# Layer 1's experts: moving where pieces of attention stand inside a batch of experts

## The chip, the core and the metric

The kernel runs on one core of one Trainium2 chip. The metric is device time in microseconds (us), from the first to the last instruction and what lies around them, for one execution of the whole two-layer program. The core has a matrix engine (PE, with weight loads shown apart as PEld), a vector engine (DVE), an activation engine (ACT), a general engine (POOL) and a queue engine (SP) that issues most transfers. Each engine takes its instructions in the order in which the program was written for it.

## The reference

The input is x, 16 x 256 tokens of 128 numbers. Each of two layers normalises x, computes attention and a mixture of experts from the same normalised x, and adds their product to x. Layer 0 has gated linear attention and 8 experts; layer 1, where the change lies, has causal softmax attention with 16 heads and 16 experts, two of them for each token:

```python
mag = jnp.einsum('td,ndh->tnh', fx, bank_mag)
freq = jnp.einsum('td,ndh->tnh', fx, bank_freq)
hidden = jnp.tanh(mag) * jnp.cos(jax.nn.softplus(freq) + 0.1 + bank_phase[None, :, :])
out_all = jnp.einsum('tnh,nhd->tnd', hidden, bank_down)
...
x = x + s * g      # s: attention of layer 1, g: silu of the weighed experts
```

## The kernel before, in words

**Experts.** Tokens are sorted by expert on the chip and padded to 79 slots of 128 rows. A slot has one expert. `experts` takes a batch of 8 slots, so there are ten batches, numbered 0 to 9 here; the last has 7. One batch goes through these steps, in program order:

1. *Turning*: two groups of four transposes (L1133) into a PSUM tile `pxt`, each copied by ACT to `xgT` (L1135).
2. *Chain stage*: for each of four pairs of slots, 8 matmuls into `pf` (L1144), three ACT steps for softplus (L1149 to L1151) and five DVE steps that bring the angle into range (L1153 to L1161).
3. *Tanh stage*: a table of activation functions is loaded (L1165); for each pair, 8 matmuls into `pm` (L1171) and a tanh (L1177); then the sines of all four pairs (L1182; the cosine's quarter turn is in the phase), and the other table is loaded back (L1183).
4. *Product stage*: tanh times cosine on DVE (L1188), the choice of each row's weight (`weigh`, L393), then two halves of 16 matmuls into `pe` (L1196), each evacuated by DVE to `og` (L1201).

**Attention as filling.** `attention` is a generator of 254 pieces, and `fill(n)` emits the next n of them at the place where it is called. The pieces are: a *score pair* (`both`; in its full form the query scores `Sq` of one block, L940 and L946, together with the key scores `Sk` of an earlier block, L979), `queries` (L1008, L1010), `weighted` (L1029), `normed` (L1041), `turned` (L1061), `projected` (L1069), and for every four blocks a `setup` of two key parts (L911), two query parts (L902) and the values (L920). Two kinds of follow-up work are put off. The DVE step of most pieces (for a score pair the row maximum, L956 or L958) waits in the list `later` and is emitted when the next piece is taken. A score pair's exponential on ACT (L986) comes as an item of its own, kind 1, just before the next piece.

In a batch the calls are: one piece between the two groups of transposes; three in each of the four pairs of the chain stage, called the first, second and third place here (after the matmuls, after the ACT steps, after the DVE steps); at most one after each group of tanh matmuls; one after the second table load; and one after each half of the products. In the tanh stage `fill(1, False)` takes nothing as long as an exponential is due, because the table for it isn't loaded:

```python
if kind == 1 and not exps:
    ahead.append((kind, f))
    return True
```

So once a score pair has been taken there, no more is taken, and its exponential runs just after the load of L1183.

**PSUM.** The score tiles have the tag `S` and two buffers: in a full score pair `Sq` takes one and `Sk` the other. The next pair's `Sq` waits for the row maximum of this one, its `Sk` for this one's exponential. The other pieces share two buffers of the tag `ps`, and everything of the experts (`pxt`, `pf`, `pm`, `pe`) two of the tag `pf`.

**Other queues.** Each call of `fill` also calls `spread`, which issues one gather of rows (`xg`, L386) or one scatter of results (`yd`, L398) on POOL; POOL also masks the exponentials (L989). The weights of the next batch (`wt`, L1116) are issued on SP after a batch has been emitted; nine buffers serve batches of eight.

**The tail.** After the ten batches the remaining results are scattered (`give`), and a loop takes three pieces of attention and one step of `weighed` (L1211 to L1227) until all eight blocks of tokens are out (`finished`, L1233 to L1235). In one round of this loop a new block's results `gg` are loaded, and the blocks before it move on by a step:

```python
while b < NB:
    fill(3)
    next(ends, None)
```

Of the kernel before, what the change touches and what calls it, by code (L numbers as in the profile page):

```python
# [38 lines left out]
FILL = 3  # L39
# [13 lines left out]
def ib(ap, n):  # L53
    s = list(ap.shape)
    return ap.unsqueeze(len(s)).to_broadcast(s + [n])
# [3 lines left out]
def two_layer_kernel(  # L59
# [331 lines left out]
    def weigh(xg, lay, j0, n):  # L391

        return nc.vector.copy_predicated(  # L393
            xg[:, :n, D], seconds[lay][:, j0 : j0 + n].bitcast(I32), xg[:, :n, D + 1]
        )
# [44 lines left out]
    def spread():  # L440

        turn[:] = [not turn[0]]
        if wanted and (turn[0] or not given):
            fetch(1)
        else:
            give(1)
# [397 lines left out]
    with ExitStack() as c1:  # L844
# [281 lines left out]
        def experts(j0, n, wts, xg, fill):  # L1126

            vs, ths, xgTs = [], [], []
            for i0 in range(0, n, 4):
                n4 = min(4, n - i0)  # L1130
                pt = pf_.tile([P, 4, P], F32, tag="pf", name="pxt")
                for i in range(n4):
                    nc.tensor.transpose(pt[:, i, :], xg[:, i0 + i, 0:D], ident)  # L1133
                xgT = hp.tile([P, 4, P], F32, tag="xgT", name="xgT", bufs=3)
                nc.scalar.copy(xgT[:, 0:n4, :], pt[:, 0:n4, :])  # L1135
                xgTs.append(xgT)
                if i0 == 0:
                    fill(1)
            for i0 in range(0, n, 2):
                m = 2 * min(2, n - i0)  # L1140
                pf = pf_.tile([P, 4, P], F32, tag="pf", name="pf")
                for k in range(m):
                    i, c = i0 + k // 2, k % 2
                    nc.tensor.matmul(  # L1144
                        pf[:, k, :], wts[i][:, c * P : (c + 1) * P], xgTs[i // 4][:, i % 4, :], start=True, stop=True
                    )
                fill(1)
                z = hp.tile([P, 4, P], F32, tag="z", name="z", bufs=2)
                nc.scalar.activation(z[:, :m, :], pf[:, :m, :], AF.Abs)  # L1149
                nc.scalar.activation(z[:, :m, :], z[:, :m, :], AF.Exp, scale=-1.0)  # L1150
                nc.scalar.activation(z[:, :m, :], z[:, :m, :], AF.Ln, bias=1.0)  # L1151
                fill(1)
                nc.vector.scalar_tensor_tensor(z[:, :m, :], pf[:, :m, :], 0.0, z[:, :m, :], ALU.max, ALU.add)  # L1153
                v = hp.tile([P, 4, P], F32, tag="v", name="vt", bufs=CPB // 2 + 1)
                for i in range(m // 2):
                    ks = slice(2 * i, 2 * i + 2)
                    nc.vector.scalar_tensor_tensor(  # L1157
                        v[:, ks, :], z[:, ks, :], INV2PI, ib(wts[i0 + i][:, WROW - 2 :], P), ALU.mult, ALU.add
                    )
                nc.vector.tensor_scalar(z[:, :m, :], v[:, :m, :], MAGIC, MAGIC, ALU.add, ALU.subtract)  # L1160
                nc.vector.tensor_tensor(v[:, :m, :], v[:, :m, :], z[:, :m, :], ALU.subtract)  # L1161
                vs.append(v)
                fill(FILL - 2)

            nc.scalar.preload_act_table_set(TRIG)  # L1165
            for i0 in range(0, n, 2):
                m = 2 * min(2, n - i0)
                pm = pf_.tile([P, 4, P], F32, tag="pf", name="pm")
                for k in range(m):
                    i, c = i0 + k // 2, k % 2  # L1170
                    nc.tensor.matmul(  # L1171
                        pm[:, k, :], wts[i][:, H1 + c * P : H1 + (c + 1) * P], xgTs[i // 4][:, i % 4, :],
                        start=True, stop=True,
                    )
                fill(1, False)
                th = hp.tile([P, 4, P], F32, tag="th", name="th", bufs=CPB // 2 + 1)
                nc.scalar.activation(th[:, :m, :], pm[:, :m, :], AF.Tanh)  # L1177
                ths.append(th)
            for i0 in range(0, n, 2):
                m = 2 * min(2, n - i0)  # L1180
                v = vs[i0 // 2]
                nc.scalar.activation(v[:, :m, :], v[:, :m, :], AF.Sin, scale=TWOPI)  # L1182
            nc.scalar.preload_act_table_set(LN_EXP)  # L1183
            fill(1)
            for i0 in range(0, n, 2):
                m = 2 * min(2, n - i0)
                v, th = vs[i0 // 2], ths[i0 // 2]
                nc.vector.tensor_tensor(th[:, :m, :], th[:, :m, :], v[:, :m, :], ALU.mult)  # L1188
            weigh(xg, 1, j0, n)
            og = hp.tile([P, n, D], F32, tag="og", name="og", bufs=1)  # L1190
            for i0 in range(0, n, 4):
                n4 = min(4, n - i0)
                pe = pf_.tile([P, 4, D], F32, tag="pf", name="pe1")
                for i in range(i0, i0 + n4):
                    for c in range(2):
                        nc.tensor.matmul(  # L1196
                            pe[:, i - i0, :], ths[i // 2][:, 2 * (i % 2) + c, :],
                            wts[i][:, 2 * H1 + c * D : 2 * H1 + (c + 1) * D], start=(c == 0), stop=(c == 1),
                        )
                fill(1)  # L1200
                nc.vector.tensor_tensor(  # L1201
                    og[:, i0 : i0 + n4, :], pe[:, 0:n4, :], ib(xg[:, i0 : i0 + n4, D], D), ALU.mult
                )
                given.extend((og, 1, j0 + i, i) for i in range(i0, i0 + n4))
# [41 lines left out]
        def fill(n, exps=True):  # L1246

            k = 0
            while k < n:
                spread()  # L1250
                kind, f = ahead.pop() if ahead else next(pieces, (3, None))
                if kind != 1:
                    while later:
                        later.pop(0)()
                if kind == 3:
                    return False
# [3 lines that stand above are left out]
                if f is not None:  # L1260
                    f()
                k += kind == 0
            return True

        ET = mybir.EngineType
        with tc.manual_schedule(engines={ET.Activation, ET.PE, ET.DVE, ET.SP}):
# [20 lines left out]
            for k, (j0, n) in enumerate(batches):  # L1287
                now, got = got, None
                if k + 1 < len(batches):
                    got = rows_of(*batches[k + 1])  # L1290
                experts(j0, n, *now, fill)
                fetch(len(wanted))
                if got:
                    got = weights_of(*batches[k + 1]), got
# [61 lines left out]
```

## Time and profile before

| what | value |
|---|---|
| median of 3 runs | 1118.82 us (1113.76 to 1123.27) |
| profiled execution, own time | 1121.9 us |
| span of its instructions | 1120.2 us |
| granted PE clock, mean over the span | 0.874 of full speed |
| first tanh-stage table load to the last batch's one | 657.3 to 1021.7 us |
| last `og` of the experts ends | 1031.9 us |

The span is the time from the first to the last instruction on the core; 1.7 us lie around it in the profiled execution. "Idle before" in a row is the time in which an engine had nothing running just before that instruction, with the instruction that released it behind the arrow. Times in a timeline count from the start of the span.

### The profile page before, as it was taken

What the parts mean: (1) busy time and instruction counts of PE and PEld (TensorE: products, weight loads), DVE (VectorE), ACT (ScalarE), POOL (GpSimd) and SP (SyncE); (2) the same over time, 40 slices, a digit from 0 to 9 for tenths busy, and PEclk for the clock granted to TensorE, in tenths of its full rate; (3) what the DMA queues carried; (4) which work ended last, traced back from release to release, by engine and by line L of the source; (5) the groups of instructions that cost most, each with busy time, mean ns of one, the idle gap of its engine ahead of it and who ended that gap; (6) DMA issues with size and microseconds to landing.
All of it is one profiled execution on the core that took longest, in us unless ns stands there. A gap on an engine that the chain in (4) does not pass through costs nothing.

```text
span 1120.2 us, 17719 instructions
## 1 busy us (share of the span) xinstructions
PE 865.9 (77%) x6394; PEld 610.8 (55%) x6394; DVE 743.6 (66%) x1384; ACT 603.8 (54%) x1101; POOL 427.4 (38%) x446
## 2 busy tenths in 40 slices
PE   5545688788888878467867789888998888879676
PEld 4323466666666666335434366665666566656343
DVE  5677456646565655355688578778777866856585
ACT  3303566757657675364313365656565565545474
POOL 2000453544443622452121526445644643532220
PEclk9987799999989899656868799999999998988866
DMA  4040478633322320310070113432442343230241
GB/s 125 1 76 1 124 182 177 136 87 88 95 75 81 93 78 18 101 57 1 1 169 35 34 50 107 138 101 66 147 135 61 113 137 92 72 102 10 85 114 37
DMA packets 88416, 95.41 MB, mean 85 GB/s; under 512 B 22229, under 2 KB 64041, under 8 KB 88329
## 3 DMA queue, kind: packets, MB, share of 16 engines
q1 hardware_dynamic: 78632, 74.32, 24.1%
q0 software_dynamic: 9696, 19.97, 6.8%
q8 instruction: 50, 0.82, 0.3%
q14 instruction: 38, 0.30, 0.1%
HBM read 78.03 MB, written 22.51 MB: 90 GB/s over the span
## 4 chain that ended last, share of the span: by engine, by line
PE 42%; DVE 27%; ACT 17%; issue 7%; DMA 3%; POOL 3%; SPq 0%; DVEq 0%; POOLq 0%; ACTq 0%
PE pq L556 4%; PE Sq L946 4%; PE pf L737 3%; PE Sk L979 3%; PE pm L1171 3%; PE pe L1196 3%; DVE negm L958 2%; DVE vt L1157 2%; PE pe L767 2%; PE yx L1029 2%; PE Sq L940 2%; ACT pr L986 2%; DVE vt L1161 2%; DVE z L1153 1%; ACT sg L742 1%
## 5 line engine op out<-in xcount | busy, mean ns | idle before, releaser
L398 POOL DMA_INDIRECT yd<-og,row x150 | 157.4, 1049 | 236.0 <-DVE og L771 123.6
L386 POOL DMA_INDIRECT xg<-xnd,tok x150 | 150.2, 1001 | 111.1 <-ACT sp L522 53.3
L989 POOL TENSOR_SCALAR_AFFINE_SELECT pr<-pr 128x1024 f32<-128x1024 f32 x64 | 74.6, 1166 | 220.8 <-ACT pr L986 220.5
L979 PE MATMUL Sk<-qm,kT 32*128 32x256 f32 x768 | 130.1, 464 | 28.4 <-DVE negm L958 25.9
L986 ACT ACTIVATE pr<-Sk 128x1024 f32<-128x1024 f32 x96 | 97.9, 1021 | 78.6 <-PE Sk L979 78.3
L946 PE MATMUL Sq<-km,qT 32*128 32x256 f32 x768 | 130.0, 458 | 8.8 <-DVE mx L956 6.9
L737 PE MATMUL pf<-xgT,wt 128*128 128x128 f32 x568 | 82.8, 293 | 26.4 <-ACT sg L745 8.6
L946 PEld LDWEIGHTS Sq<-km,qT 32*128 32x128 f32 x768 | 71.6, 209 | 56.1 <-issue 33.4
L979 PEld LDWEIGHTS Sk<-qm,kT 32*128 32x128 f32 x768 | 77.0, 216 | 42.2 <-DVE negm L958 29.1
L737 PEld LDWEIGHTS pf<-xgT,wt 128*128 128x128 f32 x568 | 75.9, 205 | 43.6 <-issue 16.4
L958 DVE TENSOR_REDUCE negm<-Sq 128x8 f32<-128x1024 f32 x64 | 78.0, 1220 | 30.6 <-PE Sq L946 16.0
L742 ACT ACTIVATE sg<-pf,nb 128x128 f32<-128x128 f32 x142 | 44.1, 362 | 61.5 <-PE pf L737 61.3
L940 PE MATMUL Sq<-mq,identb 128*128 128x512 bf16 x128 | 43.5, 425 | 22.6 <-DVE negm L958 11.0
L753 DVE SCALAR_TENSOR_TENSOR gt<-pf,nb,sg 128x128 f32<-128x128 f32 x142 | 42.4, 343 | 21.0 <-ACT sg L746 21.0
L1196 PE MATMUL pe<-wt,th 128*128 128x128 f32 x316 | 42.2, 289 | 16.7 <-DVE th L1188 16.7
L1196 PEld LDWEIGHTS pe<-wt,th 128*128 128x128 f32 x316 | 39.0, 200 | 24.1 <-DVE th L1188 13.0
L956 DVE TENSOR_REDUCE mx<-Sq 128x8 f32<-128x1024 f32 x32 | 39.0, 1218 | 13.0 <-PE Sk L979 8.5
L618 DVE COPY_PREDICATED a<-upper,pA 128x512 f32<-128x512 int32 x32 | 23.3, 729 | 35.3 <-PE pA L617 34.5
L355 ACT ACTIVATE ohj<-hi,place 128x568 bf16<-128x568 bf16 (+1 forms) x16 | 12.7, 795 | 61.8 <-DVE hi L354 58.7
L1144 PE MATMUL pf<-xgT,wt 128*128 128x128 f32 x316 | 44.4, 284 | 0.0
L1144 PEld LDWEIGHTS pf<-xgT,wt 128*128 128x128 f32 x316 | 39.8, 196 | 8.2 <-issue 8.0
L767 PE MATMUL pe<-sb_wo,gt 128*128 128x128 f32 x284 | 38.1, 287 | 7.5 <-DVE gt L753 7.2
(273 smaller groups left out, 2066.0 us busy)
## 6 DMA issues: line engine op xcount, KB each, us to landing
wt<-bank SPq DMA_DIRECT2D x79, 385.0 KB
wt<-in_w_dram SPq DMA_DIRECT2D x71, 256.0 KB
gg<-yd SPq DMA_DIRECT2D x32, 256.0 KB
xnd<-xnx SPq DMA_DIRECT2D x16, 260.0 KB
xg<-xnd,tok POOLq DMA_INDIRECT x150
yd<-og,row POOLq DMA_INDIRECT x150
x<-in_x_dram SPq DMA_DIRECT2D x8, 256.0 KB
bank<-in_freq_dram SPq DMA_DIRECT2D x1, 2048.0 KB
```

The lines of the kernel that those rows point to most:

```text
L386: return nc.gpsimd.indirect_dma_start(out=xg[:, i, :], out_offset=None, in_=xnds[lay], in_offset=bass.IndirectOffsetOnAxis(ap=toks[lay][:, ...
L398: give = nc.gpsimd.indirect_dma_start(out=yds[lay], out_offset=bass.IndirectOffsetOnAxis(ap=rows[lay][:, j : j + 1], axis=0), in_=og[:, i, ...
L737: nc.tensor.matmul(pf[:, c, :], wts[i][:, c * P : (c + 1) * P], xgT[:, i, :], start=True, stop=True)
L767: nc.tensor.matmul(pe[:, i, :], gts[i][:, c, :], sb_wo0[:, c, :], start=(c == 0), stop=(c == 1))
L940: nc.tensor.matmul(S[:, c], identb, mq, start=True, stop=False, skip_group_check=True)
L946: nc.tensor.matmul(S[:, c, js, :], qT[part][r, tq], km[r, js, tk], start=not diag, stop=True, skip_group_check=True,)
L958: passed(nc.vector.tensor_reduce(ng, S, AX.X, ALU.max, negate=True))
L979: nc.tensor.matmul(S[:, c, js, :], kT[part][r, tk], qm[r, js, :], start=True, stop=True, skip_group_check=True,)
L986: nc.scalar.activation(pr, S, AF.Exp, scale=scale)
L989: pooled(nc.gpsimd.affine_select(pr_, pr_, pattern=[[0, 8], [1, P]], compare_op=ALU.is_ge, fill=0.0, base=0, channel_multiplier=-1,))
L1144: nc.tensor.matmul(pf[:, k, :], wts[i][:, c * P : (c + 1) * P], xgTs[i // 4][:, i % 4, :], start=True, stop=True)
L1196: nc.tensor.matmul(pe[:, i - i0, :], ths[i // 2][:, 2 * (i % 2) + c, :], wts[i][:, 2 * H1 + c * D : 2 * H1 + (c + 1) * D], start=(c == 0), ...
```

## The change

Three calls of `fill` change inside `experts`. One piece is added after the first four transposes, ahead of their copy; one is added between tanh times cosine and the products' matmuls; and in the first of the four pairs of the chain stage the third place is left out. A batch thereby has one fixed place more than before. No arithmetic changes.

```diff
                 for i in range(n4):
                     nc.tensor.transpose(pt[:, i, :], xg[:, i0 + i, 0:D], ident)
+                if i0 == 0:
+                    fill(1)
                 xgT = hp.tile([P, 4, P], F32, tag="xgT", name="xgT", bufs=3)
                 nc.scalar.copy(xgT[:, 0:n4, :], pt[:, 0:n4, :])
...
                 vs.append(v)
-                fill(FILL - 2)
+                if i0:
+                    fill(FILL - 2)
...
             weigh(xg, 1, j0, n)
+            fill(1)
             og = hp.tile([P, n, D], F32, tag="og", name="og", bufs=1)
```

`FILL` is 3, so `fill(FILL - 2)` takes one piece.

## The prediction

> **What bounds the kernel now.** I read the page's busy times first, then the waits of the matrix engine between 640 and 1030 us (the experts of layer 1), then windows by stage, then the timeline around one tanh stage, and last the tail.
>
> ```profile
> PE 865.9 (77%) x6394; PEld 610.8 (55%) x6394; DVE 743.6 (66%) x1384; ACT 603.8 (54%) x1101; POOL 427.4 (38%) x446
> ```
>
> ```profile
> PE pe L1196 <- DVE th L1188: 16.7, 9, 6.7
> PE Sk L979 <- DVE negm L958: 14.6, 8, 3.1
> PE Sq L940 <- DVE mx L956: 7.3, 5, 3.2
> ```
>
> The columns are total us, times, longest. PE waits for tanh times cosine ahead of the products (nearly 1.1 us a batch, but 6.75 once), and for row maxima in the chain stage. Nine chain stages (batches 1 to 9) together, by windows:
>
> ```profile
> sum 204.40, PE 174.99 PEld 116.06 DVE 172.56 ACT 125.09 POOL 138.99; mean PE 19.44 PEld 12.90 DVE 19.17 ACT 13.90 POOL 15.44
> ```
>
> There PE is busy 86% and DVE 84%: they bound the stage together, through the short score buffers. In the tanh and product stages ACT's fixed order and then PE decide.
>
> **What moves.** I counted the pieces through the code's order, from the first piece in batch 0 that the timeline shows (`normed` at 629.81). Before, a batch takes 1 + 12 + 1 + 2 = 16 fixed pieces, and the tanh stages take 8 in all: 168, leaving 37 for the tail. After, 17 fixed ones, and 6 in the tanh stages: 176, leaving 29. So eight pieces leave the tail: a `projected`, four score pairs (two with a mask), a `queries`, a `weighted`, a `normed`.
>
> **Their work in the experts.** At full clock the timeline has a masked pair at 1.7 us of PE, an unmasked one at 1.1, `projected` 1.0, `queries` 0.9, the short `weighted` 0.9, `normed` 0.5: 3.4 + 2.2 + 1.0 + 0.9 + 0.9 + 0.5 = **8.9 us** of PE, where PE is nearly full.
>
> **The new place before the products.** Batch 2 before, ACT and then PE:
>
> ```profile
> 747.44 1.28 ACT L1183 ACT_TABLE_LOAD   x1
> 748.73 1.02 ACT L986 ACTIVATE pr<-Sk 128x1024 f32<-128x1024 f32 x1
> ```
>
> ```profile
> 746.64 2.05 PE L1196 MATMUL pe<-wt,th 128*128 128x128 f32 x16 [0.93 <-DVE th L1188]
> 748.63 0.70 PE L946 MATMUL Sq<-km,qT 32*128 32x256 f32 x4
> 749.81 0.48 PE L979 MATMUL Sk<-qm,kT 32*128 32x256 f32 x2 [0.48 <-ACT pr L986]
> ```
>
> The products start 0.8 us before the sines end, and a score pair behind them still waits 0.48 us for the exponential that stands behind the table load. With a pair ahead of the products, that wait comes 2 us earlier: PE is free at 745.7, can do 0.35 us of `Sq`, and stands until 749.8; pair and first half then end near 753.0 instead of 751.0. Products, the gathers' release and everything behind on PE queue behind it. By the count the new place holds a score pair in batches 0, 2, 3, 7 and 9, always with an exponential pending. That loses 1.9, 2.0, 2.0, 1.9 and, where nothing was idle before (batch 9: products started at once at 1027.42, the exponential ended at 1030.29), 3.3: 11.1 us. Elsewhere the piece fits the gap: batch 1 (a key part) gains 1.0, batch 4 (`weighted`) 1.5, batch 5 (`queries`) 1.1. The 6.75 us wait of batch 8 is a key part in the place after the load: its copy waits behind load and exponential on ACT, and DVE's `km` (6.36 us idle) stands ahead of tanh times cosine. After the change that key part falls into batch 6, and a query part fills 1 us of it: 2.0 gained over both. Sum: 11.1 - 5.6 = **+5.5 us**. Bounds: -5.6, if no pair had to wait, to +11.1 without the gains; I take the worked value, since batch 2's row is the very wait.
>
> Two rules of the Trainium skill bear here. "ScalarE: Activation LUTs", "What ACT_TABLE_LOAD costs", has about 1.28 us for the load and 1.38 more for a drain. The rows above show 1.28 and the next activation 0.01 us after it. By the rule each of the five pairs would wait 1.38 longer, 6.9 in all; I use the row.
>
> The second speaks of the clock. PE stands still about 3.0 us (batches 0, 7), 3.3 (9) and 3.9 (2, 3). "TensorE: Matmul & The Clock Gate", "HAM oscillation", says gaps up to about 3.4 us keep the full clock. In this trace gaps of 1.75 us (804.34 to 806.09) and 3.21 (732.49 to 735.70) were each followed by a stretch at half clock (column 0.50):
>
> ```profile
> 735.30:738.70 3.40, 3.00 (x19) 1.36 (x18) 3.30 (x6) 0.00 (x0) 1.90 (x2) 0.50 0.18 39
> 806.97:810.38 3.41, 3.41 (x23) 2.52 (x16) 3.31 (x5) 1.02 (x1) 3.00 (x3) 0.50 0.30 61
> ```
>
> Of the eleven gaps of 1.7 us or more between 640 and 1030, nine have one beside them. Each costs 3.4 / 2 = 1.7 us of PE. By the rule two of the new gaps cost 3.4 us together; by the trace five x 0.8 x 1.7 = **6.8 us**. I take the trace; ends 3.4 and 8.5.
>
> **The place left out in the chain stage.** A pair in the first place has its maximum ahead of the five DVE steps; in the second or third it comes behind them (0.68 + 2 x 0.53 + 0.50 + 0.78 = 3.0 us), and the next pair finds the buffer taken. Pairs in those two places go from 33 to 27 by the count. PE's gaps in the chain stages and the attention pieces among the tanh matmuls add up to some 39 us before; in proportion 39 x 6 / 33 = **-7.1 us**, and the half-clock stretches these gaps bring (34.1 us without batch 8's, so 17.1 lost) shrink by 17.1 x 6 / 33 = **-3.1**. This is the least certain term: nothing, if DVE's load decides (over ten batches its steps for pieces fall only from 107 to 97 us there, beside some 119 of chain steps), up to twice as much, if the short first pair lets DVE stay ahead.
>
> **The place in the turning.** PE has no wait there that a piece could fill: its `pf` matmuls show idle 0.0. ACT's wait for the transposes (33.0 us at the copy) is not on the path, since 1 to 2 us of pieces and transposes lie between the copy and its reader. An exponential now ahead of the copy is hidden by them; uncovered, it costs 1.0 us. So this place is worth 0 beyond the work counted above.
>
> **POOL, SP.** One more call of `spread` a batch brings one gather or scatter (1.0 us on a POOL that is 38% busy) forward: 0, covered by the rest of the batch. The next weights (385 KB each) are released by the products; where those start later, so do the loads, but the extra turning piece gives back 1.1 us: 0, and up to 2 us a batch if a pair of slots has to wait for its weights.
>
> **The tail.** Windows from the last `og`; the columns after the length are busy us of PE, PEld, DVE, ACT, POOL, then the clock:
>
> ```profile
> 1031.90:1046.50 14.60, 8.57 (x100) 5.49 (x97) 5.07 (x7) 3.66 (x4) 8.66 (x9) 0.98 0.27 81
> 1046.50:1096.60 50.10, 36.55 (x254) 22.74 (x255) 40.54 (x80) 33.74 (x100) 9.89 (x7) 0.70 0.34 97
> 1096.60:1105.60 9.00, 8.04 (x42) 4.01 (x38) 7.60 (x16) 7.16 (x18) 1.09 (x1) 0.50 0.15 45
> 1105.60:1120.20 14.60, 7.11 (x52) 3.83 (x52) 3.30 (x9) 2.21 (x4) 0.00 (x0) 0.73 0.09 26
> ```
>
> The first 14.6 us are seven scatters at 1.28, a landing and the first load of results; DVE stands in front of that load, whatever attention is left. This stays. The next 50.1 us are seven rounds up to the last block's sum; DVE is busy 81%. After the change these rounds hold lighter pieces (2.5 us less DVE work by the count): 47.5. The third row is the last block's way to its result; the fourth was attention alone, which now is finished in time. What then remains behind the result is two DVE steps (1.4) and the store (3.4): 4.8 instead of 14.6. The tail saves 2.6 + 9.8 = **12.4 us**.
>
> **The sum.** Experts: 8.9 + 5.5 + 6.8 - 7.1 - 3.1 = +11.0. Tail: -12.4. Net -1.4 on the profiled execution's 1121.9, that is 1120.5. It stood 3.1 above the median of the runs shown (1118.8), so the forecast for that is **1117 us**, no difference that can be told: a measurement of this kernel can tell about 1%, 11.2 us.
>
> **The rivals.** *Faster, the pieces find room*: the chain-stage relief is twice mine (-20.4) and the clock follows the 3.4 us rule (3.4): experts 8.9 + 5.5 + 3.4 - 20.4 = -2.6, tail -12.4, so 1104. For it: PE idles 57 us between 630 and 1035, far more than the pieces need. Against: 6.75 of the product wait only changes its batch, and PE is at 86%. Chance 0.20.
>
> *Slower, the exponential behind the table load*: all five stalls bring half clock (8.5), and the chain stage gives nothing back, since DVE is as loaded as before: 8.9 + 5.5 + 8.5 = +22.9, against a tail that saves 10 as its rounds stay DVE-bound: about +13, so 1132. It decides by itself once stall and clock cost the five batches 3 us each with no relief. For it: DVE's 84%. Against: six pairs fewer stand behind the chain steps. Chance 0.20.
>
> *The tail doesn't shorten*, as `weighed` alone sets its end: then 11.0 - 2.6 = +8.4 with my experts, 1127. Against: the fourth window has DVE busy 3.3 us of 14.6, after all `weighed` work. Chance 0.03.
>
> My forecast has the remaining 0.57, with a range of its own of 1108 to 1126. The whole range reaches to the rivals' centres, 1104 to 1132. Faster by over 1%: 0.21; within: 0.58; slower: 0.21.
>
> **What would show it.** The last `og` should end near 1043 in the span, and the first sum's `gg` wait end 14 to 15 us later; the last store should follow `xnx` by about 5 us. In batches 0, 2, 3, 7 and 9 `Sk` should wait about 3 us for `ACT pr L986`, a wait that totals under 1 us now. The 6.75 us wait on tanh times cosine should be in batch 6. I am wrong if those five waits are missing, if the chain stages of nine batches together differ from 204 less one piece each and the relief (about 185) by over 10 us, or if the tail still takes over 80 us.

## The result, and the profile after

The changed kernel takes 1129.33 us (median of 20 runs, 1114.39 to 1134.95), the kernel before 1120.98 (20 runs, 1113.76 to 1126.73). The ratio is 1.0050, with a 95% interval of 1.0029 to 1.0071: slower by half a per cent, where the forecast was 1117 against 1118.8, faster by 0.16%. The ratio is taken over fast runs alone, which leaves out three of the changed kernel's twenty, so it is not the quotient of the two medians. The profiled execution of the changed kernel is the fastest of its twenty, so its span of 1112.7 us is not typical, and its stages have to be read, not its end. It is 7.5 us shorter than the profile before, although the experts and the tail together are 0.5 us longer: its first `pf` matmul starts at 626.95 us, 8.0 us earlier than before (634.91), behind layer 0, which the change leaves alone.

The busy times of the page show that the same work was done, on PE at a better clock (0.887 over the span):

```profile
PE 852.0 (77%) x6394; PEld 605.8 (54%) x6394; DVE 743.8 (67%) x1384; ACT 601.8 (54%) x1101; POOL 424.8 (38%) x446
```

PE's waits in the experts (640 to 1037 us; total us, times, longest), with the line of the first wait before the change (640 to 1030 us) ahead of them:

```profile
PE Sk L979 <- ACT pr L986: 0.7, 2, 0.5
```

```profile
PE Sk L979 <- ACT pr L986: 17.4, 7, 3.6
PE Sk L979 <- DVE negm L958: 9.5, 6, 2.7
PE Sk L979 <- DVE mx L956: 8.6, 5, 3.6
PE pe L1200 <- DVE th L1191: 7.8, 4, 5.9
```

The wait for tanh times cosine fell from 16.7 to 7.8 us, of which 5.9 is the key part's, now in batch 6. A wait of 0.7 us has become one of 17.4: key scores for an exponential. Batch 2 shows where, first ACT, then PE in program order behind the last tanh matmuls:

```profile
730.42 2.18 ACT L1185 ACTIVATE vt<-vt 128x512 f32<-128x512 f32 x4
732.61 1.28 ACT L1186 ACT_TABLE_LOAD   x1
733.91 1.02 ACT L986 ACTIVATE pr<-Sk 128x1024 f32<-128x1024 f32 x1
```

```profile
730.82 0.70 PE L946 MATMUL Sq<-km,qT 32*128 32x256 f32 x4
734.99 0.80 PE L979 MATMUL Sk<-qm,kT 32*128 32x256 f32 x2 [3.46 <-ACT pr L986]
735.00 0.80 PE L946 MATMUL Sq<-km,qT 32*128 32x256 f32 x2
...
736.99 3.36 PE L1200 MATMUL pe<-wt,th 128*128 128x128 f32 x14
```

PE reaches the pair before the sines have ended, does a few query scores, and stands until the exponential behind the table load has freed its buffer; the products wait behind. When PE starts again, its matmuls take longer: 0.80 for a row that took 0.48 before. These are windows of the trace from the starts of the half clock in batches 0, 2 and 3 (columns as before: busy us of PE, PEld, DVE, ACT, POOL, then the clock):

```profile
655.40:662.20 6.80, 6.24 (x30) 5.34 (x31) 1.64 (x2) 2.00 (x3) 2.18 (x2) 0.50 0.27 82
733.90:740.70 6.80, 5.71 (x29) 4.90 (x30) 1.74 (x3) 2.05 (x2) 0.00 (x0) 0.50 0.19 58
778.30:781.70 3.40, 3.40 (x20) 2.75 (x15) 1.39 (x2) 1.02 (x1) 0.00 (x0) 0.50 0.18 14
```

The nine chain stages of batches 1 to 9 together (204.40 us before), and then the tail in the four parts of before (from the last `og` to the first block's sum, to the last block's, to its result, to the end):

```profile
sum 191.00, PE 162.53 PEld 110.46 DVE 158.99 ACT 122.16 POOL 134.62; mean PE 18.06 PEld 12.27 DVE 17.67 ACT 13.57 POOL 14.96
```

```profile
1037.00:1049.60 12.60, 11.51 (x134) 6.67 (x133) 5.53 (x9) 3.07 (x3) 9.01 (x9) 1.00 0.30 91
1049.60:1098.20 48.60, 31.58 (x201) 18.29 (x201) 35.02 (x74) 32.33 (x99) 7.35 (x5) 0.65 0.35 100
1098.20:1107.80 9.60, 2.55 (x9) 1.96 (x9) 6.22 (x15) 6.41 (x18) 0.00 (x0) 0.55 0.19 55
1107.80:1112.70 4.90, 0.00 (x0) 0.00 (x0) 1.40 (x3) 0.00 (x0) 0.00 (x0) 0.50 0.18 54
```

The last part has no PE work left, and ends 4.9 us after the last result.

### The profile page after: what moved, and what is told of

Its sections match the earlier page's. It is cut to its first block, busy times and chain, and to the rows that moved or that the text cites. A ratio compares the mean times of both kernels' runs of the same rounds, so it can differ in the third digit from the quotient of the medians.

```text
span 1112.7 us, 17724 instructions
## 1 busy us (share of the span) xinstructions
PE 852.0 (77%) x6394; PEld 605.8 (54%) x6394; DVE 743.8 (67%) x1384; ACT 601.8 (54%) x1101; POOL 424.8 (38%) x446
## 5 line engine op out<-in xcount | busy, mean ns | idle before, releaser
L979 PE MATMUL Sk<-qm,kT 32*128 32x256 f32 x768 | 121.0, 436 | 50.3 <-ACT pr L986 23.1
L946 PE MATMUL Sq<-km,qT 32*128 32x256 f32 x768 | 123.7, 436 | 9.3 <-DVE mx L956 4.3
L979 PEld LDWEIGHTS Sk<-qm,kT 32*128 32x128 f32 x768 | 71.9, 201 | 65.5 <-ACT pr L986 28.0
L946 PEld LDWEIGHTS Sq<-km,qT 32*128 32x128 f32 x768 | 66.9, 197 | 52.3 <-issue 32.1
L742 ACT ACTIVATE sg<-pf,nb 128x128 f32<-128x128 f32 x142 | 44.1, 362 | 60.0 <-PE pf L737 59.9
L1200 PE MATMUL pe<-wt,th 128*128 128x128 f32 x316 | 49.0, 319 | 7.8 <-DVE th L1191 7.8
L1200 PEld LDWEIGHTS pe<-wt,th 128*128 128x128 f32 x316 | 45.4, 229 | 14.9 <-issue 8.3
L940 PE MATMUL Sq<-mq,identb 128*128 128x512 bf16 x128 | 40.5, 400 | 7.6 <-DVE negm L958 6.7
L355 ACT ACTIVATE ohj<-hi,place 128x568 bf16<-128x568 bf16 (+1 forms) x16 | 12.7, 795 | 60.7 <-DVE hi L354 57.8
```

What stands on the lines that cost most here:

```text
L742: nc.scalar.activation(sg[:, c, :], pf[:, 2 + c, :], AF.Exp, scale=-1.0, bias=nbs[i][:, 2 + c : 3 + c])
L946: nc.tensor.matmul(S[:, c, js, :], qT[part][r, tq], km[r, js, tk], start=not diag, stop=True, skip_group_check=True,)
L979: nc.tensor.matmul(S[:, c, js, :], kT[part][r, tk], qm[r, js, :], start=True, stop=True, skip_group_check=True,)
L1200: nc.tensor.matmul(pe[:, i - i0, :], ths[i // 2][:, 2 * (i % 2) + c, :], wts[i][:, 2 * H1 + c * D : 2 * H1 + (c + 1) * D], start=(c == 0), ...
```

## The experiments

The chip of the comparison above is called A. The runs below were on four others: B (e1 to e4, e12 to e15), C (e5 to e8), D (e9 to e11) and E (e16 to e18). Each ratio is against the kernel before on the same chip at the same time. Those chips took 1165 to 1176 us for the kernel before, 4 to 5% more than A.

"Pieces" is the number that the code's order puts ahead of the tail, counted from the first piece of batch 0. "Experts" is the time from the first `pf` to the last `og`, "half clock" the time in the experts with the clock at 0.50, of which half is lost where PE has work; both from the one profiled execution, us. That execution lies up to 8.2 us from the median of its kernel's runs (15 us for the changed kernel on A), so a few us between two rows are not told apart.

| run | what is in it | pieces | ratio (95%) | experts | tail | half clock |
|---|---|---|---|---|---|---|
| before, A | | 168 | 1 | 396.9 | 88.4 | 49.2 |
| after, A | | 176 | 1.0050 (1.0029 to 1.0071) | 410.1 | 75.6 | 47.8 |
| e1 | after | 176 | 1.0215 (1.0181 to 1.0249) | 444.2 | 76.6 | 81.9 |
| e2 | after, no pairs ahead of the products | 171 | 0.9971 (0.9945 to 0.9998) | 420.6 | 77.4 | 64.9 |
| e3 | after, no place ahead of the products | 168 | 1.0042 (1.0012 to 1.0072) | 412.1 | 87.3 | 61.4 |
| e4 | before + place ahead of the products | 176 | 1.0227 (1.0184 to 1.0269) | 444.6 | 76.6 | 90.6 |
| e5 | before, C | 168 | one execution | 419.1 | 86.9 | 59.0 |
| e6 | after | 176 | 1.0139 (1.0091 to 1.0187) | 452.4 | 76.8 | 92.1 |
| e7 | after, PE kept busy ahead of the pair | 176 | 1.0073 (1.0044 to 1.0101) | 438.0 | 78.5 | 47.8 |
| e8 | before + that place without pairs | 171 | 0.9936 (0.9905 to 0.9967) | 426.3 | 77.8 | 71.7 |
| e9 | before + place in the turning | 179 | 1.0148 (1.0118 to 1.0179) | 436.7 | 73.7 | 58.0 |
| e10 | before - one chain-stage place | 155 | 0.9862 (0.9831 to 0.9894) | 382.5 | 102.7 | 42.3 |
| e11 | e8 again | 171 | 0.9948 (0.9924 to 0.9971) | 414.1 | 77.3 | 52.6 |
| e12 | after without its turning piece | 169 | 1.0064 (1.0035 to 1.0093) | 429.6 | 81.5 | 85.3 |
| e13 | before - the turning place | 155 | 0.9785 (0.9751 to 0.9819) | 375.4 | 101.5 | 40.9 |
| e14 | before - three chain-stage places | 137 | 1.0095 (1.0065 to 1.0124) | 386.1 | 128.7 | 75.0 |
| e15 | e10 + e8's place | 156 | 0.9927 (0.9898 to 0.9955) | 380.0 | 102.9 | 39.4 |
| e16 | e13, 15 pieces ahead of batch 0 | 171 | 0.9888 (0.9850 to 0.9926) | 402.9 | 79.3 | 64.9 |
| e17 | e13, 13 pieces ahead of batch 0 | 168 | 1.0321 (1.0259 to 1.0383) | 440.9 | 87.0 | 92.2 |
| e18 | before, E | 168 | one execution | 416.4 | 85.9 | 56.0 |

### Which part of the change costs (e1 to e4, e8, e11)

e1 is the changed kernel as it is. e2 lets the new place take anything but a score pair, which then stays for the next place:

```diff
             weigh(xg, 1, j0, n)
-            fill(1)
+            fill(1, pairs=False)
...
```

The lines by which `fill` knows a score pair and hands it back are left out here.

e3 has the other two edits alone, e4 the new place alone on the kernel before:

```diff
 e3
             weigh(xg, 1, j0, n)
-            fill(1)
 e4, against before
             weigh(xg, 1, j0, n)
+            fill(1)
```

e8 and e11 are e4 with `fill(1, pairs=False)`.

> The changed kernel unaltered, for a second profile: the first was of its fastest run, 15 us below its median. If the change itself costs time (stalls of score pairs behind the table load), the time is 5 to 9 us over the kernel before (ratio 1.004 to 1.008) and the profile again shows five waits of about 3 us of Sk for the exponential, in batches 0, 2, 3, 7 and 9. If the difference of the medians was chance of the chip, the ratio is 0.998 to 1.002. Where a usual run has its extra time against the first profile is open: layer 0 (which the change doesn't touch), the experts of layer 1, or the tail.

> The changed kernel, but the new place before the products takes no score pair; it then stays empty, as before the change (171 pieces in the experts, 34 in the tail). Theory A, the stall behind the table load with its half clock: 5 stalls of 3.2 us and their clock go, 5 pieces go back to the tail at some 1.2 us each, so 6 to 12 us below the changed kernel and at or under the kernel before (ratio to before 0.994 to 1.000). Theory B, PE is full and every piece taken into the experts costs its work there, stalls aside: within 3 us of the changed kernel (ratio 1.003 to 1.007).

> The changed kernel without the new place before the products: only the piece moved from the chain stage's first pair to ahead of the copy of the transposes (168 pieces in the experts and 37 in the tail, as before the change). Theory A (the product place alone costs): 3 to 8 us under the kernel before (ratio 0.993 to 0.998), since the chain stage is lighter. Theory B: the same as before, 0.998 to 1.002. Theory C, it is this move that costs, as two pieces in the turning lengthen the way to the first chain: 1.003 or more.

> The kernel before plus the new place before the products alone; the chain stage and the turning stay as they were (176 pieces in the experts, 29 in the tail, and the same pieces in the new place as in the changed kernel). Theory A: the five stalls are there and no chain stage is lightened, so 4 to 8 us over the changed kernel, ratio to before 1.007 to 1.014. Theory C (the other move costs): at or under the kernel before, 0.995 to 1.000.

> The kernel before plus the new place before the products, which takes no score pair; chain stage and turning as they were. If the move from the chain stage to the turning costs some 0.4% (as e3 had it) this is the best of all: ratio to before 0.990 to 0.997. If that move costs nothing, it is as e2: 0.995 to 1.000.

> The kernel before with the place ahead of the products that takes no score pair, a second time, to see whether its gain holds on another run and perhaps another chip. Theory A (pieces without an exponential fill the wait for tanh times cosine at no cost): ratio 0.993 to 0.997, tail about 9 us shorter. Rival (the gain of 0.6% belonged to that chip's clock): within 0.2% of before.

The new place with score pairs carries the loss: e4 has it alone and loses 2.3%, as much as the whole change on that chip; without pairs the place gains 0.5 to 0.6% on two chips (e8, e11). e3 shows that moving one piece from the chain stage to the turning, at the same 168 pieces, gains nothing: it costs 0.4%. Two expectations missed here by being too low: e1 was to lose 0.4 to 0.8% and e4 0.7 to 1.4%. From e2 to e1 and from e8 to e4 five pieces more also move into the experts, so these differences are not the stalls alone; e12 below parts the two.

### How much of it is the clock (e5 to e7)

e7 gives PE eleven 128x128 matmuls, whose result is overwritten, just ahead of the new place wherever a score pair is next there:

```diff
...
+            first = pf_.tile([P, 4, D], F32, tag="pf", name="pe1")
+            if pair_next():
+                for _ in range(11):
+                    nc.tensor.matmul(first[:, 0, :], ident, xgTs[0][:, 0, :], start=True, stop=True)
             fill(1)
...
```

`pair_next` looks ahead in the sequence without taking anything, and the first half of the products then uses the tile `first`; both are left out here.

> The kernel before unaltered, for a second profile of it, on the chip of the runs beside it: the stages of its experts (chain, tanh, product) and its half-clock time are what the others are held against. Time within 1% of the kernel before by construction.

> The changed kernel unaltered, beside the next run. Its ratio to the kernel before was 1.005 on the first chip and 1.0215 on the second; theory A (stalls and the half clock that they bring) expects 1.004 to 1.025 here, larger where the profile shows more half-clock time in the experts against the kernel before.

> The changed kernel with 11 matmuls of 128 x 128 without use (3.0 us at full clock) put ahead of the score pair in the five batches where the new place holds one, so that PE works while it would stand waiting for the exponential; the products overwrite what they write. Theory A1, half clock after the stalls is a large part of the loss: the half-clock stretches behind the five stalls go and it is 5 to 12 us below the changed kernel beside it. Theory A2, the loss is the waiting itself and the work behind it: within 3 us of the changed kernel.

The wait for the exponential in the experts, of e6 and then of e7:

```profile
PE Sk L979 <- ACT pr L986: 18.7, 8, 3.6
```

```profile
PE Sk L979 <- ACT pr L986: 4.7, 7, 1.2
```

The useless matmuls can't bring the exponential forward; they fill the same time. What they change is the clock: half-clock time in the experts falls from 92.1 to 47.8 us, the experts are 14.4 us shorter in the profile, and behind the five stalls not one whole window of half clock is left. The profiles flatter e7: e6's is of one of its slowest executions (1198.64 us) and e7's of its fastest (1177.16), and 13.8 of the 44.3 us of half clock went from the chain stages. By the medians the kernel goes from 1195.38 to 1183.63 us, 11.8 us. The ratios differ by 0.0066, 7.8 us, and their intervals overlap by 0.001. So the half clock that follows the stalls costs some 8 to 12 us here, beside 16.4 us that PE stands still in the five stalls.

### The places in the turning and in the chain stage, each alone (e9, e10, e12, e13)

```diff
 e9, against before
+                if i0 == 0:
+                    fill(1)
                 xgT = hp.tile([P, 4, P], F32, tag="xgT", name="xgT", bufs=3)
 e10, against before
-                fill(FILL - 2)
+                if i0:
+                    fill(FILL - 2)
 e13, against before
                 xgTs.append(xgT)
-                if i0 == 0:
-                    fill(1)
```

e12 is e10 with the new place ahead of the products, score pairs and all.

> The kernel before with one piece added in the turning alone (the first part of the change by itself): ten more calls move pieces from the tail into the experts, and no score pair stands ahead of the products. Theory A (the loss is the pair ahead of the products and the half clock behind its wait; work moved in costs its own matmul time and comes back in the tail): the wait of the key scores for the exponential stays under 2 us in all, the tail shortens by about 11 us, the experts lengthen by 9 to 12 us, the time is within 0.3% of before. Theory B (the moved work itself is what costs, in a matrix engine that is nearly full, stall or not): experts longer by 17 us or more, time up 0.7% or more. Theory C (pieces ahead of the products gain, pieces in the turning cost by putting the copy later): slower by about 0.4% with the experts longer by some 15.

> The kernel before with only the third place of the first pair left out (the part of the change from which the prediction took a relief of 7.1 us of waits and 3.1 us of half clock): about ten fewer places in the experts. Prediction's own theory: the experts lose the work of about ten pieces (some 10 us) and 10 us more by relief, 20 in all, while the tail grows by 10 to 13: faster by 0.6% or more. Rival (no relief, the vector engine's load decides the chain stage): experts shorter by 8 to 11 us, tail longer by as much, the time within 0.3% of before.

> The change without its piece in the turning: the place ahead of the products is there, score pairs and all, and the third place of the first pair is left out, so the experts hold 169 pieces by the code's order where the kernel before has 168. Theory S (stall and half clock): five score pairs stand ahead of the products here too, so experts some 15 to 22 us longer than before, of that 11 us of stall less the gaps filled and about 12 us of half clock, the tail 1 to 2 us shorter, slower by 1.0 to 1.7%. Theory N (the number of pieces in the experts decides, each costing more there than in the tail): within 0.3% of before, since the number is the same.

> The kernel before with the one place between the two groups of transposes left out and the chain stage as it was: 155 pieces in the experts by the count, the same number and the same sequence after the first ones as with the third place of the first pair left out (that kernel was 1.4% faster). Theory N (number of pieces): as fast as that one, 0.984 to 0.989 of before, experts shorter by 30 us or more and tail longer by 16. Theory R (relief in the chain stage by a shorter first pair, as the prediction had it): the chain stage keeps all its twelve pieces, so no more than the work of the ten pieces moves, within 0.4% of before.

e12 has five stalls of 3.1 to 3.6 us and as good as no more pieces than before, and loses 0.6%, less than the 1.0 to 1.7% expected of stall and clock. Its ten chain stages take 222.8 us, against 247.7 and 248.4 in e18 and e5 on other chips, but they also hold ten pieces fewer, so how much of that is relief is not shown. e9 has no pair ahead of the products and still loses 1.5%, so the pairs are not the only way to lose; its chain stages have 49.2 us of PE gaps, against 42.3 in e5 and 43.2 in e18, and which of its places brings them was not tried. And one place *less* gains: 1.4% in e10, 2.2% in e13, whose chain stage keeps all twelve places. So what gains there is not the place left out of the chain stage. e13 is the fastest of all that ran. Both have 155 pieces in the same sequence from batch 1 on; read through the order, no batch has a key part behind the table load. The wait for tanh times cosine in e13's experts:

```profile
PE pe L1194 <- DVE th L1186: 10.4, 10, 1.1
```

About 1.0 in each batch; the single one of 6.7 is gone. That is only part of the gain. PE's gaps in e13's experts are 43.7 us, against 65.0 in e5 and 66.6 in e18, the kernel before on other chips: some 22 us fewer, of which the long wait is 5.7. Some 15 of them are in the chain stages (27.4, against 42.3 and 43.2), which keep all their places. Why those run better is not shown, and e13's ratio of 0.9785 is lower than either theory allowed (0.984 at the least).

### Number or pattern (e14 to e18)

e14 leaves the third place out in three of four pairs (`if i0 == 6`). e15 is e10 and e8 in one. e16 and e17 are e13 with one line ahead of the loop over the batches:

```diff
+            fill(15)
             for k, (j0, n) in enumerate(batches):
```

and `fill(13)` in e17. The ten batches then hold 156 and 155 pieces, and differ in nothing but where in the sequence they begin.

> The kernel before with the third place left out in three of the four pairs of the chain stage: 137 pieces in the experts and 68 in the tail by the count. Theory N in its simple form (a piece costs 1.6 to 2.8 us in the experts and 1.2 in the tail, at any number): 31 pieces fewer, 0.965 to 0.985 of before. Theory P (what gains is the pattern: at 155 pieces every second batch has the same pieces in the same places, with no key part behind the table load, and not the number): three of the ten batches have a score-stage key part or query part behind the load again, waits for tanh times cosine come back to 12 us or more, and the time is 0.99 to 1.01 of before.

> The kernel before with the third place of the first pair left out, and the place ahead of the products added for pieces other than score pairs: the two faster versions so far in one, 156 pieces in the experts by the count, and every second batch a weighted piece ahead of the products. If both gains hold side by side (0.986 and 0.995): 0.978 to 0.985 of before. If the second gain was only the removal of the 6.75 us wait behind the key part, which the first has removed too: 0.984 to 0.989, no better than the first alone.

> The kernel before without the place between the groups of transposes (as in the 2.2% faster one), and with 15 pieces of attention emitted in one go ahead of batch 0, so that the ten batches hold 156 pieces by the count and the tail 34, three fewer than before. The same kinds of pieces stand in the same places as in the faster kernel, half a period of attention further on: behind the table load queries and projected pieces only. Theory P (the pattern of pieces on places decides): experts within 6 us of that kernel's 375 us, waits for tanh times cosine near 10 us, ratio 0.973 to 0.987, as the 15 pieces cost ahead of batch 0 about what they save in the tail. Theory N (what gains is that pieces are left to the tail): the 15 pieces have to be paid ahead of batch 0 and the tail is as short as before, still 0.975 to 0.99; told apart from P by the next kernel only.

> The same with 13 pieces in one go instead of 15: 155 pieces in the ten batches and 37 in the tail, as many as before, but two pieces out of step with the last kernel, so that batches 0, 2, 4, 6 and 8 have a key part behind the table load. Theory P: each of these five batches has the wait of about 6.7 us for tanh times cosine that one batch has in the kernel before, with half clock behind most; experts 25 to 40 us longer than in the last kernel, ratio 0.995 to 1.015. Theory N (only the number of pieces in the ten batches counts): same as the last kernel within 0.4%.

> The kernel before, unaltered, for a profile on the chip of these runs: experts 405 to 420 us, tail 86 to 89 us, one wait of 6.75 us for tanh times cosine in batch 8.

From e16 to e17 the time goes from 1161.8 to 1217.0 us. Most of it is phase, not all: of the 47.6 us between the two profiles 38.0 are in the experts, 7.8 in the tail, where e17 has 37 pieces and e16 has 34, and 1.8 ahead of the first `pf`. PE's wait for tanh times cosine, in e16 and then in e17:

```profile
PE pe L1194 <- DVE th L1186: 10.2, 10, 1.1
```

```profile
PE pe L1194 <- DVE th L1186: 33.7, 5, 6.7
```

How one such wait comes about, in batch 4 of e17, PE first, then ACT, then DVE:

```profile
889.67 1.02 PE L911 MATMUL pk<-xnT,wka 128*128 128x512 f32 x2
897.44 3.43 PE L1194 MATMUL pe<-wt,th 128*128 128x128 f32 x16 [6.74 <-DVE th L1186]
```

```profile
892.54 1.28 ACT L1181 ACT_TABLE_LOAD   x1
893.84 1.02 ACT L986 ACTIVATE pr<-Sk 128x1024 f32<-128x1024 f32 x1
894.75 0.68 ACT L913 ACTIVATE kT<-pk,hmask 128x512 f32<-128x512 f32 x1
```

```profile
895.47 1.22 DVE L915 TENSOR_SCALAR km<-kT,hmask 128x512 f32<-128x512 f32 x2 [6.16 <-ACT kT L913]
896.61 2.48 DVE L1186 TENSOR_TENSOR th<-th,vt 128x512 f32<-128x512 f32 x4
```

A key part is the piece of the place behind the load. Its copy stands on ACT behind sines, load and exponential; its `km` stands on DVE ahead of tanh times cosine and waits 6.16 us for that copy, and so the products wait 6.74. This happens in batches 0, 2, 4, 6 and 8, each time with 6.8 or 10.2 us of half clock after it, 40.8 in all. In the experts the phase does what was expected of it (25 to 40 us longer), and the number of pieces is excluded as the only cause; the kernel as a whole lost more than was expected (0.995 to 1.015). It is excluded by e14 too: 31 pieces fewer than before lose 0.9%. Its experts are some 30 us shorter than in e5 and e18, but 31 pieces more make the tail 42 us longer.

Two more expectations missed. e16's experts took 402.9 us, not within 6 of e13's 375.4: its chain stages have 44.1 us of gaps on PE, e13's 27.4, on another chip, so the gain of e13's chain stages did not come back with its pattern, and this difference stays open. And e15, which holds the edits of two faster versions, has a ratio above that of e10 (0.9927 against 0.9862), though its experts are no longer in the profile (380.0). The two ran on different chips, and one change's ratio has differed by 1.7% between chips (after and e1), so whether the second edit costs here stays open too.

## Why the prediction was wrong

Two terms failed. The relief of the chain stage was no price per place: predicted at -10.2 us, it was about -10 in A's one profile, nearly all of it clock, and about +11.5 on C. The half clock behind the stalls was too small: 6.8 us predicted, 11.9 measured. The measured 1129.3 lies outside the forecast's own range of 1108 to 1126.

**What held, on the profile of chip A.** The stalls came in batches 0, 2, 3, 7 and 9 as counted: 3.14, 3.46, 3.60, 3.14 and 3.08 us. The long wait moved to batch 6 (5.89). Work: I take from the experts' 13.2 us the change of PE's gaps (54.1 to 58.7) and half of the change of half-clock time; 9.3 us remain for PE's work, 8.9 were predicted. The gaps outside the chain stages grew by 6.2 (21.2 to 27.4; predicted 5.5). The tail saved 12.7 (predicted 12.4), its last part being 4.9 us (4.8). The load cost 1.28 and the exponential came 0.02 us after it, so the drain of 1.38 us that the Trainium skill adds ("ScalarE: Activation LUTs", "What ACT_TABLE_LOAD costs") is not seen here either.

**The clock after the stalls was undersized.** The step was "five x 0.8 x 1.7 = 6.8 us", one window of 3.4 us of half clock behind each of four stalls in five. Each of the five had a window, and two of the five a double one: 6.83, 6.83, 3.41, 3.41 and 3.41, 23.9 us in all on chip A, and as much in e6. That loses 11.9 us; e7 got 8 to 12 back. The trace before showed the larger price already: of the nine stretches beside its eleven gaps six lasted 3.41 us, two 6.83 and one 10.24, 44.4 us in all. That is 2.0 us lost for each gap, some 10 for five stalls. Three of the new gaps (3.08, 3.14, 3.14) would pass the rule "no PE-idle gaps >~3.4µs" of the Trainium skill ("TensorE: Matmul & The Clock Gate", "HAM oscillation"); the trace was the right one to follow, but a window is not always one.

**The relief of the chain stage was not a price per place.** The step was "in proportion 39 x 6 / 33 = -7.1 us", with 3.1 us of clock in its train. The chain stages of all ten batches, from the first `pf` matmul of a batch to its first `pm`, taken apart, and beside them the rest of the experts:

| us | before, A | after, A | e5, before, C | e6, after, C |
|---|---|---|---|---|
| chain stages, length | 230.2 | 211.1 | 248.4 | 248.3 |
| PE's gaps in them | 32.9 | 31.3 | 42.3 | 49.4 |
| half clock in them | 34.0 | 17.1 | 44.5 | 53.3 |
| rest of the experts, length | 166.7 | 199.0 | 170.7 | 204.1 |

Outside the chain stages the change costs the same on both chips, 32.3 and 33.4 us. The chain stages give back 19.2 on A and nothing on C, though they hold one piece less in each batch. For the nine stages of batches 1 to 9, e5 and then e6, the trace of C has:

```profile
sum 222.60, PE 183.92 PEld 120.42 DVE 171.51 ACT 125.28 POOL 142.19; mean PE 20.44 PEld 13.38 DVE 19.06 ACT 13.92 POOL 15.80
```

```profile
sum 222.10, PE 177.68 PEld 116.93 DVE 163.14 ACT 124.26 POOL 137.51; mean PE 19.74 PEld 12.99 DVE 18.13 ACT 13.81 POOL 15.28
```

The gaps did not shrink by 7.1: 1.5 us less on A, 7.1 more on C. Half clock fell on A in its one profiled execution, by 16.9 us, and rose by 8.8 on C. My test for this step, the nine stages' length of 191 against the expected 185, held on A only through that clock. On C the step's error is 7.1 + 4.4 against the predicted -10.2: 22 us, as much as the whole error of the experts there (+33.3 against +11.0; the other terms' errors about cancel). e3 tried the step nearly by itself: with the piece moved to the turning, at 168 pieces, the pairs in the second and third places fall from 33 to 28 by the count, and the kernel lost 0.4%. Nor do the gaps follow that count elsewhere: 28 such pairs in e16 and 35 in e17, on one chip, leave 44.1 and 44.9 us of gaps. What does set them was not found.

On A itself only the fastest run was profiled; which stage made the others some 15 us longer was not seen. Their granted clock is on record, 0.861 in the mean of the nineteen against 0.887, so they had more half clock, and the relief by the clock that the profile shows need not be theirs.

**The moved piece was priced by its own work.** The forecast set 8.9 us of work in the experts against 12.4 in the tail, with the five stalls and one long wait as the only places where it mattered which piece fell where. e16 and e17 show 38 us in the experts between two phases of the same sequence. The prediction read the sequence only in two places, behind the load and ahead of the products, and in the chain stage took a mean over pieces; a change that adds one place to 16 gives every later place another piece. How much of this change's loss comes from that, beside the two terms above, was not measured.

**The rivals.** The slower one had the right two mechanisms, stalls with more half clock and no relief; its 22.9 us more in the experts lie between A's 13.2 and C's 33.3. Its 1132 is near A's 1129.3. The faster one ("the pieces find room") is refuted for this change: the chain stage's gaps did not fall as it needed.

## What to carry to other kernels

When one piece more or less is taken in a loop that draws work from a running sequence, write the new sequence out for all iterations and look at what kind falls on each dear place; between e16 and e17 that was worth 38 us in the experts, far more than the price of a piece. Ahead of the work that the stage waits for, put no piece whose buffer is freed behind a pending table load, and none whose own next step stands behind that load. And price a stall of the matrix engine of 3 us with the half clock behind it, which here cost another 1.6 to 2.4 us for each (8 to 12 us for five in e7).

## What was not expected of the hardware

The half-clock stretches lie on a grid: those that begin within the experts last 3.41, 6.83 or 10.24 us in every profile, and their starts (655.40, 733.91, 778.28 on chip A) are 23 and 13 times 3.41 us apart. Where a gap falls on this grid may decide whether it brings one or two windows; that was not tried.

The same kernel took 1121 us on one chip and 1165 to 1176 on four others. Of the 53.2 us between the profiles before on A and C, 32.5 lie ahead of the first `pf` and 22.2 in the experts, while the tail is 1.5 shorter. In the experts before, PE's gaps were 54.1 us on A and 65.0 on C, half clock 49.2 and 59.0. With it the loss of the same change went from 0.5 to 1.4 and 2.15%. What makes the chips differ stays open.
